# A graph network on one core: a sort's products one step behind their one-hots, and a gather loop in written order

## The chip, the core and the metric

The kernel runs on one core of a Trainium2 chip. The metric is the time of one launch in device microseconds, shown as the median of several runs. The engines are named as in the profile: PE (TensorE matmuls; PEld its weight loads), DVE (VectorE), ACT (ScalarE), POOL (GpSimd, which here issues the indirect DMAs), SP (SyncE, which issues most other DMAs). Each engine works through a queue of its own in a fixed order and waits on semaphores for the others.

## What is computed

A network of eight layers over 6250 nodes of 256 features and 100,000 edges (131,072 in one layer). Only the two layers around the change matter. Layer 3 adds up, for each node, a transformed feature row of every neighbour:

```python
def _L1_gnn_ref(vertex_features, edge_index, w0, w1):
    w0_features = vertex_features @ w0
    w1_features = vertex_features @ w1
    dst, src = (edge_index[0], edge_index[1])
    messages = w1_features[src]
    neighbours = jax.ops.segment_sum(messages, dst, num_segments=vertex_features.shape[0])
    return jax.nn.relu(w0_features + neighbours)
```

Layer 1 is an attention over the same edges (a softmax over each node's incoming edges), and layer 4 a graph attention over another list of 131,072 edges. The edges of layers 3 and 4 come in an order that does not suit the sums, so the kernel sorts each list by blocks of 128 nodes ("buckets") while an earlier layer runs.

## The kernel before

**The program.** `build` calls the eight stages one after the other. A scheduler orders the instructions of PE, DVE, ACT and SP from its own cost model; inside a `manual_schedule` block the engines named there keep the order in which the source writes them. Before the change such blocks stand around the loops of stages 1 and 5 and name POOL alone (`ORDERED`, L35); stage 3 has none.

**The sort, `bucket_move` (from L147).** It is a generator: each `yield` ends a step, and the stage that hosts it calls `next` (its "tick") between pieces of its own work. The sort of layer 3's edges (`sb`, 125 partitions x 800 columns) rides on stage 1, whose loop goes over 112 windows of 896 edges; the sort of layer 4's edges (`sc`, 128 x 1024) rides on stage 3. Its parts:
- Preparation: keys and values are loaded and cut into parts of 7 and 10 bits (one step).
- Counts (L223 to L229): the columns go in halves of 512 (L212). For each of 49 buckets DVE makes a 0/1 tile `isb` of 512 columns (L217, two buffers) and PE adds it into one row of `cnt` (L225).
- Positions (L297 to L310): for each bucket and half, DVE makes `isb`, PE forms three products into the PSUM tile `small` (L302 to L304, two buffers), and DVE copies the result into `pos` where the key fits (L307), one step late.
- Products (L333 to L351), in groups of 114 or 115 columns: for each 6 (`sc`) or 4 (`sb`) columns DVE makes the one-hots `ol` (L339) and `orr` (L341), multiplies the values into `orr` (L344, two instructions), and PE forms one product for each column into `mv` (L347). `ol` and `orr` have two buffers. Between groups `mv` is turned into rows, and POOL scatters them to DRAM (`scatter`, L326), 16 DMAs a group, one a step.
- The end (from L394): the sorted list is read back in pieces of 128 rows, turned by PE (L407) and written to `sl`, which the stage that uses the list reads.

**Stage 3 (`stage3`, from L1062).** A first loop computes `wd`, the neighbours' rows, as three bf16 parts, and `acc`. The second loop (L1097 to L1115) goes over 448 chunks of 256 edges. A chunk has one bucket b, which DVE's sequencer loads into a register eight at a time (`buckets`, L638). For a chunk, POOL issues two gathers of 128 rows (L630 through `gather`, tile `row3`, six buffers); PE adds the rows to the lanes of their nodes by six products with the one-hots `sel` (L1112, tile `nbp`, two PSUM buffers); DVE adds the result to `acc` (L1115). `sel` is made by DVE for four chunks at a time (L1103, two buffers). Each pass of the loop begins with one step of the sort. Behind the loop the remaining steps run, and DVE adds relu(acc) to X, 49 instructions.

Of the kernel before, what the change touches and what calls it, by code (L numbers as in the profile page):

```python
# [8 lines left out]
F = mybir.dt.float32  # L9
# [11 lines left out]
D = 256  # L21
# [13 lines left out]
ORDERED = {mybir.EngineType.Pool}  # L35
TOKG = [(g * 4, min(4, NT - g * 4)) for g in range((NT + 3) // 4)]
# [11 lines left out]
class Kern:  # L48
# [98 lines left out]
    def bucket_move(self, cx, keep, nm, key, oth, E, clamp=None, BT=6):  # L147
# [149 lines left out]
        held = None  # L297
        for b in range(NT):
            for h, n in halves:
                q = isb(b, h, n)  # L300
                big = small()
                nc.tensor.matmul(big[:, :n], bef, q, start=True, stop=False)  # L302
                for j in range(2):
                    nc.tensor.matmul(big[:, :n], idt[:NT, j, b:b + 1].to_broadcast([NT, 128]),  # L304
                                     first[:, j, h:h + n], start=False, stop=(j == 1))
                if held is not None:
                    nc.vector.copy_predicated(*held)  # L307
                held = (pos[:, h:h + n], q.bitcast(I16), big[:, :n])
                yield
        nc.vector.copy_predicated(*held)  # L310
# [22 lines left out]
        for g, c0, n in groups:  # L333
            mv = pp.tile([128, 2, W], F, name="mv")
            for c in range(c0, c0 + n, BT):
                k = min(BT, c0 + n - c)
                spread = lambda v, m: v[:, c:c + k].unsqueeze(1).to_broadcast([128, m, k])
# [8 lines left out]
                for i in range(k):  # L346
                    nc.tensor.matmul(mv, ol[:, :, i], orr[:, 0:2, :, i], start=(c + i == c0),  # L347
                                     stop=(c + i == c0 + n - 1))
# [1771 lines left out]
```

## Time and profile before

| what | us |
|---|---|
| median of 3 runs | 11024.03 |
| lowest, highest | 10996.14, 11024.14 |
| the profiled execution's own time | 10998.23 |
| its span | 10996.5 |
| stage 1's windows, first to last gather | 388.6 to 2274.6 |
| stage 3's loop, first gather to last add | 3527.1 to 5057.4 |
| stage 4's attention loop, first to last gather | 5181.2 to 7016.1 |

Busy time over the span: PE 6591.2 us (60%), PEld 4291.3 (39%), DVE 5176.0 (47%), POOL 4554.3 (41%), ACT 2132.4 (19%). No engine is full over the span, since the stages have different limits; a stage must be read by itself. In a line of a group of instructions the first number behind the bar is the group's busy time, the second the mean length of one in ns, and behind the next bar stands how long the engine was idle just before them and what ended the wait. "issue" means that nothing which the profile shows was waited for, "remote" that what ended the wait isn't told.

### The profile page before, as it was taken

The numbers are of one execution on the slowest core, as the hardware profiler recorded it, in microseconds if no ns is written. First come the engines' busy times: TensorE is split into PE (matmuls) and PEld (weight loads), VectorE is DVE, ScalarE is ACT, GpSimd is POOL, SyncE is SP. The second block draws the span as 40 slices with busy tenths as digits, with TensorE's granted clock in tenths as the row PEclk, the third lists the DMA queues.
The fourth block names the chain that finished last, engine by engine and source line by source line (L and its number), as shares of the span: only waits on it lengthen the run. The fifth ranks groups of instructions, "written<-read, shape, count | busy, mean of one in ns | idle before, by whom it ended". The sixth has DMA issues, their size and how long they took to land. (4 is left out here: it accounts for less than half of the span.)

```text
span 10996.5 us, 110782 instructions
## 1 busy us (share of the span) xinstructions
PE 6591.2 (60%) x33267; PEld 4291.3 (39%) x33267; DVE 5176.0 (47%) x14399; ACT 2132.4 (19%) x6797; POOL 4554.3 (41%) x4496
## 2 busy tenths in 40 slices
PE   4787767524784776664555556496455652742494
PEld 1344445413662333333233333275244441531363
DVE  5568855466314455543555555512333337333304
ACT  1243346420232000000111111122111110211120
POOL 0245656410133666773444444124266661243211
PEclk9888778765897776665565556588777785776597
DMA  3443356532662443343000000055444442452222
GB/s 129 150 135 110 108 154 195 152 113 90 197 200 94 136 121 100 105 115 75 7 7 6 6 7 7 4 189 179 112 118 118 123 115 75 147 161 49 53 74 69
DMA packets 613968, 1128.65 MB, mean 103 GB/s; under 512 B 156477, under 2 KB 420222, under 8 KB 599270
## 3 DMA queue, kind: packets, MB, share of 16 engines
q0 software_dynamic: 234752, 600.59, 20.7%
q1 hardware_dynamic: 320167, 454.29, 13.7%
q10 hardware_dynamic: 58412, 66.25, 2.0%
q8 instruction: 281, 4.60, 0.2%
q14 instruction: 356, 2.92, 0.1%
HBM read 930.96 MB, written 189.76 MB: 102 GB/s over the span
## 5 line engine op out<-in xcount | busy, mean ns | idle before, releaser
L765 PE MATMUL ops<-roww,ow 128*128 128x260 f32 (+1 forms) x3136 | 1025.1, 476 | 480.8 <-issue 236.7
L630 POOL DMA_INDIRECT roww<-kvd,saidx x784 | 843.2, 1076 | 1023.5 <-PE small L225 385.9
L630 POOL DMA_INDIRECT row<-gatd,scsl x864 | 834.6, 966 | 1001.4 <-issue 220.7
L630 POOL DMA_INDIRECT row<-w1d,sbsl x896 | 892.4, 996 | 568.8 <-PE nbp L1112 178.4
L630 POOL DMA_INDIRECT roww<-zd,saidx x784 | 811.1, 1035 | 587.0 <-issue 220.9
L765 PEld LDWEIGHTS ops<-roww,ow 128*128 128x128 f32 x3136 | 712.9, 242 | 690.0 <-issue 276.0
L1112 PE MATMUL nbp<-row,sel 128*128 128x256 bf16 x2688 | 576.9, 364 | 329.3 <-DMA row<-w1d,sbsl 201.1
L753 ACT ACTIVATE roww<-roww,pw 128x64 f32<-128x64 f32 x3136 | 758.4, 333 | 18.1 <-issue 15.6
L1514 DVE TENSOR_REDUCE Mc<-P 128x4 f32<-128x1024 f32 x432 | 520.7, 1221 | 375.0 <-remote 221.1
L347 PE MATMUL mv<-orr,ol 128*128 128x234 f16 (+1 forms) x1824 | 545.8, 445 | 216.1 <-DVE orr L344 171.3
L1029 PE MATMUL qe<-qw,ohT 128*128 128x256 bf16 x2352 | 424.5, 319 | 303.7 <-DVE roww L1032 214.7
L1112 PEld LDWEIGHTS <-sel 128*128 128x128 bf16 x2688 | 371.1, 155 | 583.7 <-issue 325.6
L1510 PE MATMUL P<-identb,mb 128*128 128x512 bf16 x864 | 470.2, 566 | 166.7 <-issue 86.8
L1351 PE MATMUL yp<-wr,hr 128*128 128x256 f32 x2176 | 537.8, 387 | 52.7 <-DVE yr L1354 52.4
L1389 PE MATMUL hp<-xr,wr 128*128 128x256 f32 x2176 | 535.3, 398 | 28.4 <-ACT hr L1391 18.0
L1354 DVE TENSOR_TENSOR yr<-yp,br 128x256 f32<-128x256 f32 x328 | 138.8, 424 | 862.4 <-PE yp L1351 797.5
L1148 PE MATMUL tps<-ident,xn 128*128 128x128 f32 x490 | 125.5, 404 | 686.3 <-DVE xn L125 470.7
L1513 PE MATMUL P<-rb,sel 96*128 96x512 bf16 x864 | 468.5, 565 | 88.2 <-DVE rb L1504 70.5
L1032 DVE TENSOR_TENSOR roww<-roww,qe 128x512 f32<-128x512 f32 x448 | 270.3, 612 | 399.5 <-DMA roww<-kvd,saidx 166.2
L1389 PEld LDWEIGHTS hp<-xr,wr 128*128 128x128 f32 x2176 | 400.3, 196 | 143.5 <-ACT hr L1391 28.0
L1351 PEld LDWEIGHTS yp<-wr,hr 128*128 128x128 f32 x2176 | 408.9, 194 | 109.0 <-DVE yr L1354 57.6
L1115 DVE TENSOR_TENSOR acc<-acc,nbp 128x256 f32 x448 | 187.2, 418 | 523.3 <-PE nbp L1112 313.1
(587 smaller groups left out, 12967.4 us busy)
## 6 DMA issues: line engine op xcount, KB each, us to landing
wr<-in_moe_dram SPq DMA_DIRECT2D x108, 1026.0 KB
lr<-salaned SPq DMA_DIRECT2D x112, 448.0 KB
yd<-yr SPq DMA_DIRECT2D x164, 256.0 KB
wr<-in_moe_dram SPq DMA_DIRECT2D x56, 513.0 KB
eat<-in_edge_attr_dram ACTq DMA_DIRECT2D x32, 781.2 KB
qw<-qd SPq DMA_DIRECT2D x112, 192.0 KB
br<-in_L_ffn_b_dram SPq DMA_DIRECT2D x164, 128.0 KB
main<-osb SPq DMA_DIRECT2D x112, 129.0 KB
```

Source lines behind the costliest of these rows:

```text
L347: nc.tensor.matmul(mv, ol[:, :, i], orr[:, 0:2, :, i], start=(c + i == c0), stop=(c + i == c0 + n - 1))
L630: return self.nc.gpsimd.indirect_dma_start(out=out, out_offset=None, in_=table, in_offset=bass.IndirectOffsetOnAxis(ap=idx, axis=0))
L753: nc.scalar.activation(x, x, AF.Copy, scale=p[:, j, i * H + h:i * H + h + 1])
L765: nc.tensor.matmul(ps[:, :VW], ow[:, j, :], row[:, j, v0:v0 + VW], start=(j == 0), stop=(j == BW - 1))
L1029: nc.tensor.matmul(ps[:, b], ohT[:, j + b, :], qw[:, k], start=(k == 0), stop=(k == 2))
L1032: nc.vector.tensor_mul(kr, kr, ps[:, :m])
L1112: nc.tensor.matmul(ps, sel[:, :, 2 * (c % G) + k], row[:, j * D:(j + 1) * D], start=(k + j == 0), stop=(k == 1 and j == 2))
L1351: nc.tensor.matmul(yp, hT[:, k, i * 128:(i + 1) * 128], w[:, O2 + k * D:O2 + (k + 1) * D], start=(k == 0), stop=(k == KH - 1))
L1389: nc.tensor.matmul(hp, w[:, k * H + m * 128:k * H + (m + 1) * 128], xe[:, k], start=(k == 0), stop=(k == 1))
L1510: nc.tensor.matmul(P[:, k], mb[:, :, 2 * i + k], self.identb.unsqueeze(1).to_broadcast([128, 4, 128]), start=True, stop=False)
L1513: nc.tensor.matmul(P[:, k], sel[:, 2 * i + k, :], rb, start=False, stop=True)
L1514: nc.vector.tensor_reduce(mg[:, i, :], P.rearrange("p k h e -> p h k e"), AX.XY, ALU.max)
```

## The change

Four edits go together.

The sort's products stand one step behind their one-hots. In the counts two buckets' one-hots are made in a step and multiplied in the next; in the positions PE's three products follow a step behind `isb`, and DVE's copy another step behind; in the groups `moved` issues the products of the step before. `isb` gets three buffers and the halves are equal (400 + 400 columns for `sb`, where they were 512 + 288). There are two more steps in the positions and one more in each group.

Stage 3's loop stands in a `manual_schedule` block that names POOL, PE, DVE and ACT. In a pass it now issues the chunk's two gathers, loads the buckets, lets the sort do a step, forms the six products, and then adds the sums of the chunk before (`held`). `sel` is made in the second pass of the four before those that use it (`hot`).

A row tile holds both gathers of a chunk and has five buffers: ten gathers where there were six.

```diff
+ORDER3 = ORDERED | {mybir.EngineType.PE, mybir.EngineType.DVE, mybir.EngineType.Activation}
...
-        halves = [(h, min(512, C - h)) for h in range(0, C, 512)]
+        HW = -(-C // -(-C // 512))
+        halves = [(h, min(HW, C - h)) for h in range(0, C, HW)]
...
-            q = wp.tile([128, 512], H16, name="isb")
+            q = wp.tile([128, HW], H16, name="isb", bufs=3)
...
-            for b in range(NT):
-                nc.tensor.matmul(big[:NT, :n], ko[:, NT - 1 - b:2 * NT - 1 - b], isb(b, h, n),
-                                 start=(b == 0), stop=(b == NT - 1))
-                if b % 2:
-                    yield
+            due = []
+            for b in range(NT + 1):
+                if len(due) > 1 or b == NT:
+                    for a, q in due:
+                        nc.tensor.matmul(big[:NT, :n], ko[:, NT - 1 - a:2 * NT - 1 - a], q,
+                                         start=(a == 0), stop=(a == NT - 1))
+                    due = []
+                if b < NT:
+                    due.append((b, isb(b, h, n)))
+                    if b % 2:
+                        yield
...
-        held = None
-        for b in range(NT):
-            for h, n in halves:
-                q = isb(b, h, n)
+        held, due = None, None
+        for b, h, n in [(b, h, n) for b in range(NT) for h, n in halves] + 2 * [(NT, 0, 0)]:
+            if held is not None:
+                nc.vector.copy_predicated(*held)
+                held = None
+            if due is not None:
+                a, i, m, q = due
                 big = small()
...
+                held = (pos[:, i:i + m], q.bitcast(I16), big[:, :m])
+            due = (b, h, n, isb(b, h, n)) if b < NT else None
+            yield
...
+            def moved():
+                for i in range(due[3]):
+                    at = due[2] + i
+                    nc.tensor.matmul(mv, due[0][:, :, i], due[1][:, 0:2, :, i], start=(at == c0),
+                                     stop=(at == c0 + n - 1))
+
             for c in range(c0, c0 + n, BT):
                 k = min(BT, c0 + n - c)
+                if due is not None:
+                    moved()
...
-                for i in range(k):
-                    nc.tensor.matmul(mv, ol[:, :, i], orr[:, 0:2, :, i], start=(c + i == c0),
-                                     stop=(c + i == c0 + n - 1))
+                due = (ol, orr, c, k)
                 if c > c0:
                     scatter(1)
                 yield
+            moved()
+            yield
...
-                gp = cx.enter_context(tc.tile_pool(name="s3g", bufs=6))
+                gp = cx.enter_context(tc.tile_pool(name="s3g", bufs=5))
...
+                with tc.manual_schedule(engines=ORDER3):
+                    nxt, held = hot(0), None
+                    for c in range(NCH):
+                        if c % G == 0:
+                            sel = nxt
+                        row = gp.tile([128, 2, 3 * D], BF, name="row3")
+                        for k in range(2):
+                            self.gather(row[:, k, :], wdf, S["idx"][:, 2 * c + k, 0:1])
+                        b = self.buckets(S, c)
+                        next(steps, None)
+                        ps = pp.tile([128, D], F, name="nbp")
+                        for k in range(2):
+                            for j in range(3):
+                                nc.tensor.matmul(ps, sel[:, :, 2 * (c % G) + k], row[:, k, j * D:(j + 1) * D],
+                                                 start=(k + j == 0), stop=(k == 1 and j == 2))
+                        if held is not None:
+                            add(*held)
+                        held = (ps, b)
+                        if c % G == 1:
+                            nxt = hot(c - 1 + G)
+                    add(*held)
+                    for _ in steps:
+                        pass
```

`hot(c)` makes the `sel` of four chunks as L1103 did, `add(ps, b)` adds a chunk's sums to `acc` as L1115 did.

More of the change, by code (lines that the diff above doesn't have):

```diff
@@ L295, in bucket_move @@
         yield
-        held = None
-        for b in range(NT):
-            for h, n in halves:
-                q = isb(b, h, n)
+        held, due = None, None
[5 more added lines that the diff above has]
+                a, i, m, q = due
                 big = small()
-                nc.tensor.matmul(big[:, :n], bef, q, start=True, stop=False)
+                nc.tensor.matmul(big[:, :m], bef, q, start=True, stop=False)
                 for j in range(2):
[L304 to L310, printed above, removed]
+                    nc.tensor.matmul(big[:, :m], idt[:NT, j, a:a + 1].to_broadcast([NT, 128]),
+                                     first[:, j, i:i + m], start=False, stop=(j == 1))
+                held = (pos[:, i:i + m], q.bitcast(I16), big[:, :m])
+            due = (b, h, n, isb(b, h, n)) if b < NT else None
+            yield
         nc.vector.tensor_copy(ki, pos)
@@ L334, in bucket_move @@
             mv = pp.tile([128, 2, W], F, name="mv")
+            due = None
+            def moved():
[3 more added lines that the diff above has]
+                                     stop=(at == c0 + n - 1))
             for c in range(c0, c0 + n, BT):
                 k = min(BT, c0 + n - c)
+                if due is not None:
+                    moved()
                 spread = lambda v, m: v[:, c:c + k].unsqueeze(1).to_broadcast([128, m, k])
@@ L1096, in stage3, with hot @@
                 steps = routes(cx)
-                for c in range(NCH):
-                    next(steps, None)
-                    b = self.buckets(S, c)
-                    if c % G == 0:
-                        n = 2 * min(G, NCH - c)
-                        sel = sp.tile([128, 128, 2 * G], BF, name="sel")
-                        nc.vector.tensor_tensor(
-                            sel[:, :, :n], iog[:, :, :n],
-                            locb[:, 2 * c:2 * c + n].unsqueeze(1).to_broadcast([128, 128, n]),
-                            ALU.is_equal)
-                    ps = pp.tile([128, D], F, name="nbp")
-                    for k in range(2):
-                        row = gp.tile([128, 3 * D], BF, name="row3")
-                        self.gather(row, wdf, S["idx"][:, 2 * c + k, 0:1])
-                        for j in range(3):
-                            nc.tensor.matmul(ps, sel[:, :, 2 * (c % G) + k], row[:, j * D:(j + 1) * D],
-                                             start=(k + j == 0), stop=(k == 1 and j == 2))
+                def hot(c):
+                    if c >= NCH:
+                        return None
+                    n = 2 * min(G, NCH - c)
+                    sel = sp.tile([128, 128, 2 * G], BF, name="sel")
+                    nc.vector.tensor_tensor(
+                        sel[:, :, :n], iog[:, :, :n],
+                        locb[:, 2 * c:2 * c + n].unsqueeze(1).to_broadcast([128, 128, n]), ALU.is_equal)
+                    return sel
@@ L1114, in stage3, with add @@
+                def add(ps, b):
                     ab = acc[:, ds(b, 1), :].rearrange("p o d -> p (o d)")
                     nc.vector.tensor_add(ab, ab, ps)
-                for _ in steps:
-                    pass
+                with tc.manual_schedule(engines=ORDER3):
[21 more added lines that the diff above has]
+                        pass
```

## The prediction

> **What bounds the kernel now.** I read the list of groups first, then stage 3 alone (its loop over 448 chunks runs from the first gather at 3527.05 us to the last add at 5057.4 us, 1530.4 us of a span of 10996.5 us), stage by stage, and then a few microseconds of its timeline. The groups inside the loop (line, engine, operation, count; then busy us, mean ns of one; then the engine's idle time before them and what ended it):
>
> ```profile
> L630 POOL DMA_INDIRECT row<-w1d,sbsl x896 | 892.4, 996 | 568.8 <-PE nbp L1112 178.4 <-issue 165.8 <-DVE ko L177 137.8
> L347 PE MATMUL mv<-orr,ol 128*128 128x234 f16 x1024 | 347.3, 493 | 93.3 <-DVE orr L344 59.2 <-issue 31.5 <-DVE acc L1115 2.3
> L1115 DVE TENSOR_TENSOR acc<-acc,nbp 128x256 f32 x448 | 187.2, 418 | 523.3 <-PE nbp L1112 313.1 <-remote 127.0 <-issue 41.5
> L326 POOL DMA_INDIRECT scsld<-vt,ti x144 | 153.1, 1063 | 43.9 <-issue 42.3 <-DVE orr L344 0.6 <-DVE acc L1115 0.3
> ```
>
> POOL issues 1,040 indirect DMAs here, and no engine has more work in a row: 892.4 + 153.1 us. (The 137.8 us wait lies before the loop.) Next the four parts of the loop: the sort's counts, its positions, its products, and the rest. Columns: length; busy us and instructions of PE, PEld, DVE, ACT, POOL; granted clock; DMA share; GB/s.
>
> ```profile
> 3527.00:3700.00 173.00, 116.96 (x465) 55.20 (x465) 80.93 (x243) 1.18 (x2) 122.90 (x122) 0.72 0.50 144
> 3700.00:3965.00 265.00, 203.28 (x832) 92.22 (x832) 136.27 (x299) 0.00 (x0) 175.06 (x183) 0.74 0.49 137
> 3965.00:4850.00 885.00, 615.88 (x2491) 338.21 (x2490) 478.08 (x1075) 4.95 (x18) 619.59 (x606) 0.65 0.38 104
> 4850.00:5062.00 212.00, 104.62 (x399) 59.45 (x399) 51.14 (x150) 0.00 (x0) 128.72 (x133) 0.50 0.60 124
> ```
>
> The timeline of the products shows how the time beside that work is lost:
>
> ```profile
> 4309.02 0.95 POOL L630 DMA_INDIRECT row<-w1d,sbsl  x1 [0.30 <-issue]
> 4310.27 0.95 POOL L630 DMA_INDIRECT row<-w1d,sbsl  x1 [0.30 <-issue]
> 4310.99 0.56 DVE L339 TENSOR_TENSOR ol<-iot,rl 128x768 f16<-128x768 f16 x1 [1.42 <-PE mv L347]
> 4311.90 0.68 DVE L1103 TENSOR_TENSOR sel<-iog,locb 128x1024 bf16<-128x1024 bf16 x1
> 4312.64 1.93 PE L1112 MATMUL nbp<-row,sel 128*128 128x256 bf16 x8 [0.92 <-DVE sel L1103]
> 4313.77 0.96 POOL L630 DMA_INDIRECT row<-w1d,sbsl  x1 [2.56 <-PE nbp L1112]
> ```
>
> Undisturbed gathers follow each other with 0.30 us between them (first two lines). Then DVE waits for PE's products to free a one-hot buffer, so sel comes late, so PE's sums come late, so no row buffer is free, and POOL, the engine with most to do, stands 2.56 us. With 0.30 us on each of POOL's instructions its own need is, part by part, 122.9 + 36.6 = 159.5 of 173; 175.06 + 54.9 = 230.0 of 265; 619.59 + 181.8 = 801.4 of 885; 128.72 + 39.9 = 168.6 of 212: together 1359.5, and 175.5 us in which it stands.
>
> **Part 1: stage 3 in written order, ten row buffers, adds one chunk late.** No instruction of the loop's work is taken away or added: 896 gathers, 144 scatters, 2,688 sums, 1,024 products, 448 adds and 112 sels stand in the built order of both. What can go is POOL's 175.5 us. Is anything else near POOL's pace? In the product part a step with a scatter costs POOL 2 x (470.53/466 + 0.30) + 1.063 + 0.30 = 3.98 us, one without 2.62 us (16 of a group's 26 steps have one). DVE needs 0.555 (ol) + 3 x 0.52 (orr) + 0.42 (acc) + 0.68/4 (sel) = 2.7 us. PE needs 2.08 us for six products (as at 4305.22) and 0.84 us (fast clock, 4307.11) to 1.44 us (slow clock, 4946.90) for six sums: 2.9 to 3.5 us. In the written order each PE step reads one-hots made a step earlier, and DVE's add reads sums made a chunk earlier; no wait has its releaser in the same step. PE's queue is products of step s-1, sums of chunk c; behind a late row wait only the next step's products, and for these DVE's next-but-one one-hots. So POOL sets the pace there. I take 75 of its 83.6 us. In the positions POOL needs 2 x (0.957 + 0.30) = 2.5 us a chunk and PE 3 x 0.48 + 0.84 to 1.44 = 2.3 to 2.9 us against 2.9 us now (265/91): PE is as near as POOL, and I take 18 of 35. In the opening I take 7 of 13.5. In the last part 9.2 us of the 43.4 are the way from the last gather to the last add, which stays; DMA share reaches 0.80 in the last 60 us at 109 GB/s, where deeper buffers may not help; I take 20 of the other 34. Sum: 75 + 18 + 7 + 20 = **120 us**.
>
> The wait that no view shows is POOL's wait with ten row buffers. Lower bound: only the product part's waits for PE sums go, 77.2 - 93 x 0.30 = 49 us. Upper: all but the last 9.2 us, 166 us. 120 is nearer the upper one because 104 us (178.4 - 248 x 0.30) of all the standing is put down to PE's sums directly, and 15 us more to other PE groups.
>
> Ten buffers hold about five chunks, 12.5 us of gathers, where six held 7.5. They must cover stalls such as this one, in which PE and DVE both stood for lack of something the profile does not name:
>
> ```profile
> 4547.30 0.42 DVE L1115 TENSOR_TENSOR acc<-acc,nbp 128x256 f32 x1 [10.88 <-remote]
> 4548.65 2.05 PE L347 MATMUL mv<-orr,ol 128*128 128x234 f16 x6 [9.49 <-issue]
> 4548.99 0.94 POOL L630 DMA_INDIRECT row<-w1d,sbsl  x1 [3.05 <-issue]
> ```
>
> A 10.9 us stall costs POOL 3.05 us with six buffers and should cost nothing with ten. If the rows come late for another reason, this cover is gone and the lower bound holds.
>
> Gathers beside more DVE work may be longer. The rows don't say so: with DVE 47, 51, 54 and 24% busy in the four parts, one gather (the first and last with a few other instructions among them) took 122.9/122 = 1.007, 0.957, 1.010 and 128.72/133 = 0.968 us. If all were at 1.010 the 896 would cost 0.014 us each over their mean of 0.996, 13 us; I take 5.
>
> The Trainium skill (SBUF — State Buffer, section Who interferes with whom) speaks against a denser DVE: a DVE instruction in a two-port mode shuts POOL out for its whole length, and POOL then can't write its descriptors. Taken to the letter for this loop's one-source 16-bit one-hots, 196 isb x 0.28 us, up to 55 us of POOL time would be at stake, but they are there before as well, so the sum by the rule would not change.
>
> **Part 2: the sort has more steps.** Before: 1 + 48 + 4 + 98 + 1 + 9 x 25 + 4 + 4 + 9 x 7 = 448, one for each chunk. After: positions 100, groups 26: 459. Eleven steps run behind the last chunk: about ten DVE operations of 0.28 us and two transposes on PE, among them the last of scsl. They stand among the 48 adds into X; **+3 us**, 0 to 8. In stage 1 nine steps more end the sort about one window later; it ends at 1582 us there and nobody reads it before stage 3: 0. At the start of the loop the first add stands behind ten DVE operations of 0.7 to 1.2 us and PE's third chunk behind it; POOL has ten buffers to fill in that time: 0, or 8 us without that cover.
>
> **Part 3: the same lag in stage 1.** There the sort rides on 57 of 112 windows. The 690 us of its products, in the columns of above, and two lines of their waits (us in all, times, longest us):
>
> ```profile
> 790.00:1480.00 690.00, 485.13 (x2721) 324.56 (x2718) 548.08 (x1213) 259.50 (x1028) 404.81 (x314) 0.79 0.40 111
> PE mv L347 <- DVE orr L344: 112.0, 60, 12.9
> DVE ol L339 <- PE mv L347: 12.4, 18, 3.3
> ```
>
> DVE is 79% busy and PE waits for DVE, hardly the reverse. A PE that is a step late frees PE, not DVE. What DVE can gain is its own 12.4 us; the 112 us of PE count only where PE is behind. The other engines keep the scheduler's order, and in the built program PE's products stand no further behind DVE's one-hots than before. **-10 us**, between +20 and -40. Halves of 400 + 400 for 512 + 288 are the same columns: 0.
>
> **Part 4: what the scheduler re-draws.** The built order also differs in stage 4 (its inputs scsl are ready later in the scheduler's eyes). No instruction is added. Its reductions idle 375 us in 432 calls; a tenth either way is +-37 us; I take 0.
>
> **Sum.** Against the profiled execution's 10998.23 us: -120 + 5 + 3 - 10 = -122, so 10876 us. That execution lies 26 us below the median of the runs shown (11024.03; lowest 10996.14). I forecast **10880 us** for the median.
>
> **The rivals.**
> (A) *Half the gain*: PE takes POOL's place. Its weight loads waited 325.6 + 217.8 us for "issue", which no buffer of rows mends, and at the slow clock it needs 2.9 us in the positions and 3.5 us in the products. For: clock 0.65 in the products. Against: 3.98 us on POOL where scatters go. Time: 49 us of stage 3, none of stage 1: 10998 - 49 + 8 = 10957. Chance 0.17.
> (B) *All of it*: POOL never stands (166), stage 1 gives 30: 10805. Chance 0.08.
> (C) *Nothing*: the sums wait for rows in flight (201.1 us put down to the row DMA), so the order in which they are awaited does not matter. Against it, POOL's waits are put down to PE's sums and not to DMAs. 10990. Chance 0.09.
> (D) *Slower*: the unnamed stalls grow. DVE's "remote" waits over 1 us are 40, 162.9 us in all; if they are supply that queues behind gathers in flight, ten rows in flight for six could double them, and in written order a stalled DVE soon stops PE too. Then -122 + 163 = +41: 11039. It decides from a growth of 95% on (155 us, to be 33 over). Chance 0.08.
> My forecast: 0.58.
>
> **How the numbers follow.** What a measurement of this kernel can tell from no change is about 0.3%, 33 us. Faster: forecast, A and B, 0.83. Same: C, 0.09. Slower: D, 0.08. My forecast's own range is 10835 to 10930 (the re-drawn stages). To leave out no more than 0.2 it reaches up over A to 10975 and down to B's 10800.
>
> **What would show it.** Right: the loop's length near 1410 us; POOL's gathers idle mostly 0.30 us each and waits for PE's sums well below 60 us; the product part near 3.5 us a chunk, not 3.8. Part 2: scsl's last writes among the adds into X. Part 3: the window rate in stage 1 as before. Wrong: PE's sums with no gap before them at a clock of 0.5 (A); DVE "remote" or PE "issue" waits far over 163 and 108 us (D); stage 4 longer or shorter by over 37 us.

## The result and the profile after

The changed kernel takes 11162.2 us (median of four runs, 11155.05 to 11181.94) against 11024.08 us (four runs, 10996.14 to 11027.43): 1.0134 times as long, 95% interval 1.0112 to 1.0156. Forecast were 10880 us. The profiled execution took 11155.05 us, its span is 11153.3 us, 157 us more than before. By stages (first to last gather; for stage 3 to the last add):

| stage | before, us | after, us | change | forecast |
|---|---|---|---|---|
| 1, windows | 388.6 to 2274.6 (1886.0) | 389.0 to 2417.9 (2028.9) | +143 | -10 |
| 3, loop | 1530.4 | 1526.0 | -4 | -120 |
| 4, attention loop | 5181.2 to 7016.1 (1835) | 5327.0 to 7172.9 (1846) | +11 | 0 |

Nearly the whole loss lies in stage 1, where a gain of 10 us was forecast, and the gain of stage 3 did not come. The groups of after that answer to those shown of before (columns as there; the second line counts both sorts):

```profile
L650 POOL DMA_INDIRECT row<-w1d,sbsl x896 | 890.6, 994 | 535.5 <-issue 229.9 <-DVE pos L194 138.5 <-remote 105.4
L350 PE MATMUL mv<-orr,ol 128*128 128x234 f16 (+1 forms) x1824 | 549.4, 444 | 276.8 <-DVE orr L364 210.5 <-issue 62.7 <-DVE roww L1052 2.9
L1130 DVE TENSOR_TENSOR acc<-acc,nbp 128x256 f32 x448 | 186.8, 417 | 462.7 <-remote 235.8 <-PE nbp L1146 123.1 <-PE small L316 36.1
L336 POOL DMA_INDIRECT scsld<-vt,ti x144 | 154.0, 1070 | 66.2 <-issue 41.7 <-DVE ti L408 23.5 <-DVE outp L406 0.7
```

In the first line PE's sums no longer stand among the releasers, where 178.4 us were put down to them; "remote" stands there now with 105.4 us. In the third, DVE's adds wait 123.1 us for PE's sums, not 313.1, and 235.8 us for "remote", not 127.0. The waits went from a name to no name and the loop kept its length. Products and scatters are as long as before (444 and 1070 ns; 445 over both sorts and 1063 before). The loop's four parts after (counts, positions, products, rest):

```profile
3673.60:3831.40 157.80, 92.46 (x411) 45.06 (x412) 64.99 (x205) 1.18 (x2) 105.15 (x109) 0.73 0.49 137
3831.40:4122.50 291.10, 218.81 (x907) 101.21 (x906) 152.27 (x341) 0.00 (x0) 194.90 (x203) 0.70 0.49 137
4122.50:4970.00 847.50, 573.91 (x2419) 321.89 (x2418) 475.71 (x1039) 4.39 (x16) 599.34 (x580) 0.67 0.39 106
4970.00:5200.00 230.00, 105.01 (x451) 66.04 (x450) 58.36 (x155) 0.55 (x2) 145.97 (x150) 0.55 0.58 119
```

The parts begin at other chunks, so they are compared per chunk: counts 2.89 us before and 2.92 after, positions 2.90 and 2.88, products 3.79 and 3.75, the rest 3.35 and 3.43. With 0.30 us on each instruction POOL's need is 137.9, 255.8, 773.3 and 191.0 us; it stands for the other 168.4 us, where it stood 175.5 us before.

In stage 1 the same stretch of time, 1600 to 1950 us, where the sort is over and the windows run alone. Before:

```profile
1600.00:1950.00 350.00, 264.77 (x1654) 177.86 (x1654) 194.47 (x284) 226.47 (x921) 215.53 (x204) 0.88 0.65 199
```

And after:

```profile
1600.00:1950.00 350.00, 201.43 (x1225) 145.26 (x1223) 152.59 (x218) 169.89 (x680) 142.81 (x145) 0.77 0.48 147
```

POOL issues 145 gathers where it issued 204, seven a window: 16.9 us a window for 12.0. No engine is more than 58% busy and the DMA share is lower than before, so the time goes into waiting for one another. Window 56 of 112, a little behind the sort's end, begins at 1511.8 us after and 1509.3 us before; the loss is in the windows behind it, and window by window in these eight-window means (us a window):

| windows | 56-64 | 64-72 | 72-80 | 80-88 | 88-96 | 96-104 | 104-112 |
|---|---|---|---|---|---|---|---|
| before | 12.36 | 11.20 | 12.36 | 12.66 | 14.22 | 16.89 | 17.15 |
| after | 12.49 | 16.59 | 16.98 | 17.11 | 17.02 | 17.10 | 17.14 |

Windows 64 to 96 lose 8 x (5.39 + 4.62 + 4.45 + 2.80) = 138 us. Before, too, the last windows run at 17 us.

The sort's products in stage 1 after, first the stretch and then two lines of its waits (us in all, times, longest us):

```profile
790.00:1480.00 690.00, 453.03 (x2556) 301.44 (x2554) 510.12 (x1118) 245.09 (x963) 372.83 (x299) 0.77 0.38 105
```

```profile
PE mv L350 <- DVE orr L364: 117.6, 56, 14.3
DVE ol L359 <- PE mv L350: 24.2, 16, 9.9
```

The wait of DVE that the lag was to remove grew from 12.4 to 24.2 us; PE's stayed (112.0, 117.6). The lag gained nothing in these two waits.

**The order behind the 17 us.** Where the windows run alone, the programs as built differ in where the scheduler put PE's work. PE makes, for each pair of windows, 42 products of rows (qe, L1049), 28 turns, and 14 sums (ops, L785; the profile records each as two matmuls, so the x14 below is one window's seven sums) of an earlier pair. Counted in the traces, with the pairs numbered from 0: in the quick order the sums of pair p's first window end behind 18 of the 42 row products of pair p + 2, and the second window's begin behind 41 of them. In the slow order they stand behind 7 and 21 row products of pair p + 3. Six row tiles (`rows=6`) hold three pairs, so a window of pair p + 3 can gather its rows only when the sums of pair p have freed a tile: in the slow order the second window's sums wait for rows whose place the first window's sums have only just freed. The slow order holds in pairs 46 to 52 before and in pairs 31 to 52 after, with mixed forms in the two pairs ahead of each; the expectations below count 9 and 27 pairs where the traces show these 7 and 22. What it does (the timeline of after, one turn):

```profile
2016.96 0.39 ACT L790 ACTIVATE osb<-ops 128x260 f32<-128x260 f32 x1 [1.39 <-PE ops L785]
2017.19 0.94 POOL L650 DMA_INDIRECT roww<-kvd,saidx  x1 [7.81 <-PE ops L785]
...
2017.37 0.26 SPq L814 DMA_DIRECT2D main<-osb  x1
...
2024.75 0.94 POOL L650 DMA_INDIRECT roww<-kvd,saidx  x1 [0.30 <-issue]
2025.95 0.69 DVE L1052 TENSOR_TENSOR roww<-roww,qe 128x512 f32<-128x512 f32 x1 [7.33 <-DMA roww<-kvd,saidx]
2026.70 1.46 PE L1049 MATMUL qe<-qw,ohT 128*128 128x256 bf16 x6 [9.23 <-DVE roww L1052]
...
2029.10 4.72 PE L785 MATMUL ops<-roww,ow 128*128 128x260 f32 x14
...
2033.86 0.39 ACT L790 ACTIVATE osb<-ops 128x260 f32<-128x260 f32 x1 [15.66 <-PE ops L785]
...
2034.56 1.21 POOL L650 DMA_INDIRECT roww<-kvd,saidx  x1 [8.87 <-ACT osb L790]
```

It is a ring: sums end, row buffers come free and POOL issues seven gathers (2017.19 to 2025.7); DVE has stood 7.33 us for these rows, PE 9.23 us for DVE; then come the row products, then the sums, and only then the next gathers. A turn is one window; POOL stands 8.87 us of its 17.

### The profile page after: what moved, and what is told of

Read it like the earlier page. It is cut to its first block, busy times and chain, and to the rows that moved or that the text cites. A ratio compares the mean times of both kernels' runs of the same rounds, so it can differ in the third digit from the quotient of the medians.

```text
span 11153.3 us, 110204 instructions
## 1 busy us (share of the span) xinstructions
PE 6536.9 (59%) x33267; PEld 4302.8 (39%) x33267; DVE 5194.2 (47%) x14399; ACT 2139.0 (19%) x6797; POOL 4526.8 (41%) x4496
## 3 DMA queue, kind: packets, MB, share of 16 engines
q14 instruction: 353, 2.89, 0.1%
## 5 line engine op out<-in xcount | busy, mean ns | idle before, releaser
L785 PE MATMUL ops<-roww,ow 128*128 128x260 f32 (+1 forms) x3136 | 1040.7, 481 | 463.5 <-issue 257.5
L650 POOL DMA_INDIRECT roww<-kvd,saidx x784 | 820.4, 1046 | 1142.3 <-PE small L231 386.3
L785 PEld LDWEIGHTS ops<-roww,ow 128*128 128x128 f32 x3136 | 726.9, 247 | 661.0 <-issue 281.6
L1146 PE MATMUL nbp<-row,sel 128*128 128x256 bf16 x2688 | 538.9, 351 | 340.8 <-DVE acc L1130 174.0
L1049 PE MATMUL qe<-qw,ohT 128*128 128x256 bf16 x2352 | 439.8, 323 | 487.0 <-DVE roww L1052 334.4
L1049 PEld LDWEIGHTS <-ohT 128*128 128x128 bf16 x2352 | 254.9, 114 | 653.8 <-issue 343.0
## 6 DMA issues: line engine op xcount, KB each, us to landing
main<-osb SPq DMA_DIRECT2D x112, 129.0 KB
```

The source lines that it names most:

```text
L650: return self.nc.gpsimd.indirect_dma_start(out=out, out_offset=None, in_=table, in_offset=bass.IndirectOffsetOnAxis(ap=idx, axis=0))
L785: nc.tensor.matmul(ps[:, :VW], ow[:, j, :], row[:, j, v0:v0 + VW], start=(j == 0), stop=(j == BW - 1))
L1049: nc.tensor.matmul(ps[:, b], ohT[:, j + b, :], qw[:, k], start=(k == 0), stop=(k == 2))
L1146: nc.tensor.matmul(ps, sel[:, :, 2 * (c % G) + k], row[:, k, j * D:(j + 1) * D], start=(k + j == 0), stop=(k == 1 and j == 2))
```

## The experiments

The runs were made in groups; each group ran on one chip beside runs of the kernel before, so a ratio is comparable within its group. The kernel before took 11139.02 and 11133.17 us in the groups on one chip, and 10188.44, 10199.26 and 10192.35 us on three others. "Pace" is the time of a window in stage 1 behind the sort (windows 64 to 88).

**Which edit slows stage 1: the lag or an order?** Three kernels, each the changed one but for one edit (before: 11139.02 us). The first has the old sort, without the lag, in stage 1:

```diff
-    K.stage1(by_dst, lambda cx: K.bucket_move(cx, K.keep, "sb", A["src"], A["dst"], E0, BT=4))
+    K.stage1(by_dst, lambda cx: K.bucket_move_old(cx, K.keep, "sb", A["src"], A["dst"], E0, BT=4))
```

> The changed kernel, with the sort on stage 1 in its old form (no lag, halves 512 + 288, two isb buffers); stage 3 as changed. Theory Order: stage 1 lost its 143 us not to the lag itself but to the order of PE's queue, in which the window sums (ops) stand behind the next windows' qe products. In the built order of this kernel 23 of 56 pairs of windows (30 to 52) stand so, against 9 in the kernel before and 27 in the changed one; a pair in that order costs 2 x 4.7 us more, so 11024 + 14 x 9.4 = about 11155 us. Theory Lag: the sort's late products themselves hold up stage 1; with the old sort it is as before, and with stage 3 at -4 us the kernel takes about 11020 us.

Measured: 11293.44 us, 1.013 (1.0093 to 1.0167), pace 17.06 us. The loss stays without the lag in stage 1.

The second has stage 3's loop of before, with six buffers and no block, and keeps the new sort:

```diff
-                with tc.manual_schedule(engines=ORDER3):
-                    nxt, held = hot(0), None
...
+                for c in range(NCH):
+                    next(steps, None)
```

> The changed kernel with stage 3's loop as it was before (scheduler's order, six single-row buffers); both sorts with the lag. Theory Order: only 8 pairs of windows in stage 1 (45 to 52) have the slow order in the built program; 14 more stand in an order of a third kind, in which the sums come between the qe products of the next pair. If that is as fast as before, about 11020 us; at most 11024 + 14 x 9.4 = 11155 us if it is as slow. Theory Lag: the lag is in here, so stage 1 is 143 us longer: about 11165 us.

Measured: 11202.07 us, 1.0053 (1.0035 to 1.0072), pace 13.8 to 15.7 us: a third order, between the two, with a smaller loss. So the edits in stage 3 alone move stage 1, two stages earlier in the program, and the new sort without stage 3's block moves it too.

The third takes PE's order in stage 1 out of the scheduler's hands:

```diff
-            with tc.manual_schedule(engines=ORDERED):
+            with tc.manual_schedule(engines=ORDERED | {mybir.EngineType.PE}):
                 self.att_windows(cx, S, kvd, 512, 4, 256, load, front, main, part, ends, rows=6, steps=steps)
```

> The changed kernel, and in stage 1 PE's instructions stand in the order of the source too. Then every pair has the sums of the pair before between the two windows' qe products. Theory Order: no pair pays the 4.7 us a window of the slow order, so from 11162 us 27 pairs x 9.4 = 254 us go, about 10910 us (10880 to 10960), and the windows after the sort run at 12.3 us or less to the end. Theory Lag, or that the windows are held by something else than PE's order (rows that land late, DVE): 11130 us or more.

Measured: 11318.4 us, 1.0161 (1.0119 to 1.0203). Missed. The order was not the one that the expectation names: in the trace all 14 sums of a pair stand behind all 42 row products of the next, and PE waits for ACT between the two windows' sums (6.24 us at 2026.84). Alone the windows take 15.4 us; that this order is the reason was not tested. Beside the sort they are slower: window 56 begins at 1630.6 us, and at 1552.0 us with the old sort on the same chip.

**What re-draws it?** (before: 10188.44 us.) The first is the kernel before with its own loop of stage 3 inside a block that names DVE alone:

```diff
-                for c in range(NCH):
-                    next(steps, None)
...
+                with tc.manual_schedule(engines={mybir.EngineType.DVE}):
+                    for c in range(NCH):
+                        next(steps, None)
```

> The kernel before, and one thing more: stage 3's loop stands in a manual_schedule block that names DVE alone. Nothing of stage 1, of the sorts or of the buffers is edited. In the built program pairs 30 to 52 of stage 1's windows then have the slow order on PE (the held windows' sums behind 27 and 41 of the next pair's 42 qe products; before this began at pair 44). Theory Order: the windows 60 to 88 run at 17.05 us instead of 12.4, so 14 pairs x 9.4 = +132 us, ratio 1.012 (1.009 to 1.015). Theory Lag (stage 1 lost its time to the sort's late products): stage 1 as before, ratio 1.000 (0.996 to 1.004).

Measured: 10371.67 us, 1.0179 (1.0158 to 1.02). Stage 1's windows take 1874.5 us, at a pace of 16.97 to 17.07 us. Stage 3's loop is longer too, 1468.4 us against 1416.5 us in the order of before on that chip (from the trace of the kernel below with sums written earlier in stage 1), which was not expected; so the ratio is above the range that stage 1 accounts for.

The second is the changed kernel with the old sort in stage 1 and without DVE in stage 3's block:

```diff
-                with tc.manual_schedule(engines=ORDER3):
+                with tc.manual_schedule(engines=ORDERED | {mybir.EngineType.PE, mybir.EngineType.Activation}):
```

> The changed kernel with stage 1's sort in its old form, and DVE is not named in stage 3's block (Pool, PE and ACT are). In the built program stage 1's PE order is that of the kernel before, pair by pair. Theory Order: stage 1 as before, ratio 1.000 (0.996 to 1.004), with stage 3 at 1510 to 1550 us. If stage 1's loss came from the ten row buffers, the written order of PE or the lag in the other sort, the windows after the sort stay at 17 us: ratio 1.013.

Measured: 10175.41 us, 0.9989 (0.9979 to 0.9999); stage 1 takes 1738.2 us at 12.3 to 12.6 us, as forecast; stage 3 takes 1397.2 us, well under the 1510 to 1550 expected. The same 200 us of both, first with DVE named:

```profile
1558.00:1758.00 200.00, 113.93 (x676) 83.30 (x677) 82.82 (x119) 93.44 (x375) 79.96 (x81) 0.74 0.47 141
```

And without:

```profile
1558.00:1758.00 200.00, 145.13 (x926) 98.69 (x925) 111.98 (x164) 126.08 (x514) 121.96 (x115) 0.88 0.63 195
```

81 gathers against 115, and 136 us of stage 1 between the two (1874.5 and 1738.2 us). The second run names POOL, PE and ACT in stage 3's block and has the ten buffers and stage 3's new sort, and in its trace PE's order of sums and row products in the windows alone is, pair for pair, that of the kernel before; so none of these needs to move stage 1. From the kernel with the old sort in stage 1 above, which has a pace of 17.06 us on another chip, it differs by the name DVE alone. Why the scheduler draws an earlier stage otherwise when DVE is named later stays open: its inner workings were not looked into.

**Do earlier sums help?** (same group.) If the slow order's fault is that sums stand late, sums put early should give more than the quick order. Two ways, on the kernel before: with a higher priority for the scheduler, and written earlier.

```diff
+                with tc.high_priority():
-                weigh(held)
-                scaled(held, 0)
+                    weigh(held)
+                    scaled(held, 0)
...
+                with tc.high_priority():
-                for i in range(held["n"]):
-                    sums(held, i)
+                    for i in range(held["n"]):
+                        sums(held, i)
```

> The kernel before, with the scheduler's priority raised for the held pair's weights, scalings and sums in stage 1 (weigh, scaled of the first window, sums); same instructions. In the built order the first window's sums then stand behind about 14 to 24 of the next pair's qe products and the last ones behind 36 at most. Theory Order: no pair has the slow order (9 had it), the windows go at 12.4 us or less to the end: 9 x 9.4 = -85 us, ratio 0.992 (0.988 to 0.996). If the 17 us of the last pairs has another cause (rows, the end of the sort): ratio 1.000 or more.

```diff
                 scaled(held, 0)
+                sums(held, 0)
...
                     scaled(held, 1)
-                for i in range(held["n"]):
-                    sums(held, i)
+                    sums(held, 1)
```

> The kernel before, with the first held window's sums written ahead of the next qe products and the second's right behind its scalings; no priority is raised, same instructions. In the built order the sums of both windows stand spread among the next pair's 30 qe products, the last ones behind 36 at most in the last pairs. Theory Order: ratio 0.992 (0.988 to 0.997), as with the raised priority. Otherwise 1.000 or more.

Measured: 10319.34 us, 1.0134 (1.0104 to 1.0164), and 10198.3 us, 1.0003 (0.9989 to 1.0018). Both missed. The pace is 11.8 to 12.7 us, as before, and the last pairs are slow in both (15.6 to 16.6 us). In the traces the pairs up to 41 and 43 have the first window's sums end behind 14 row products of pair p + 2 with the priority and behind 26 when written earlier (18 before), and the last pairs stay in a slow order in both, so neither run shows what an early order to the end would give. With the priority stage 1 took 1776.0 us, 37 more than the 1739.3 of the other, in an execution of 10253.22 us that lies 66 us under its median; where its remaining loss lies was not followed up.

**What holds the ring up?** In the landing records of after's slow turns 15 of a gather's 16 parts land within some 1 us, and the sixteenth 2.0 us later (both medians, windows 64 to 87). At the same time the store of the sums is on the way (from the list of DMA issues of after):

```profile
main<-osb SPq DMA_DIRECT2D x112, 129.0 KB
```

129.0 KB are 127 rows of 1040 bytes, and its records stand one behind the other, some 18 per us, some 7 us for all. The Trainium skill (DMA: Bandwidth & Descriptors, section "Why a DMA increments its semaphore by 16 and not by 1") says that a DMA uses the largest number of engines up to 16 that divides the slowest dimension of both of its sides, one for 127 partitions. The records agree: the rows of the store follow each other at 44 ns and take 47 ns each (medians), which is one at a time. The edit splits the store into 112 and 15 rows:

```diff
-                nc.sync.dma_start(main[1:NP + 128, :][ds(r[i], 127), :], o[1:128])
+                nc.sync.dma_start(main[1:NP + 128, :][ds(r[i], 112), :], o[1:113])
+                nc.sync.dma_start(main[113:NP + 128, :][ds(r[i], 15), :], o[113:128])
```

Three kernels have it (before: 11133.17 us): the changed one, the one before, and the changed one with the old sort in stage 1 and without DVE named.

> The changed kernel, but each window's 127 rows of sums go to DRAM in two DMAs of 112 and 15 rows instead of one of 127 (stages 1 and 5, 112 windows each). PE's order in the built program is that of the changed kernel. Theory Chain: in the slow order the next rows are gathered only when a window's sums are done, and are waited for at once; the store of these sums starts at the same moment, its 1040-byte packets run in one row of 17 in a microsecond (so one of the DMA engines does all 127), and the last of the 16 parts of each gather lands 2.1 to 2.4 us behind the fifteenth. With the store spread, the first wait for rows shortens by that: 17.05 us a window becomes 14.5 to 15.5, over some 54 windows 80 to 130 us, ratio to the kernel before 1.002 to 1.008 instead of 1.0134. If the late sixteenth part has nothing to do with the store, or the rows are not on the chain: 1.011 to 1.016.

> The kernel before with the same split store. Theory Chain: its last 22 windows are in the slow order, 2 us less each, 45 us, and the others and stage 5's 112 windows gain something between 0 and 1 us each: ratio 0.990 to 0.997. Otherwise 1.000, or more if the 224 further DMA issues on SP stand in the way of its loads.

> The split store on the version with the old sort in stage 1 and DVE not named in stage 3's block (0.9989 of the kernel before without the split). If both gains add: ratio 0.988 to 0.996, the fastest so far. Otherwise 0.999.

Measured: 11239.71 us, 1.0085 (1.0068 to 1.0102), pace 15.8 to 16.2 us; 11110.39 us, 0.9985 (0.9972 to 0.9998), pace 11.6 to 11.9; 11048.71 us, 0.9922 (0.9903 to 0.994), pace 11.5. The sixteenth part now lands 0.1 us behind the others, so the store was what delayed it. In the slow order that gave 0.9 us a window where 1.5 to 2.5 had been expected, and the ratio missed its range (1.002 to 1.008); the second's ratio missed too (0.990 to 0.997). The store was a part of the ring, not its cause. Only the second has a kernel without the split in its own group; the other two gains compare ratios of different chips.

**Why did stage 3 not gain?** First, if PE's sums at a low clock hold it, a third of them should show (group of 11139.02 us):

```diff
                         for k in range(2):
-                            for j in range(3):
-                                nc.tensor.matmul(ps, sel[:, :, 2 * (c % G) + k], row[:, k, j * D:(j + 1) * D],
-                                                 start=(k + j == 0), stop=(k == 1 and j == 2))
+                            nc.tensor.matmul(ps, sel[:, :, 2 * (c % G) + k], row[:, k, 0:D],
+                                             start=(k == 0), stop=(k == 1))
```

> The changed kernel, but stage 3 adds up only the first of the three bf16 parts of each gathered row: two products a chunk where there were six; gathers, adds and sort are the same. Theory Clock: stage 3's loop is bounded by PE at the clock that it is granted (0.69 of full in this loop, with a stop of PE of 3 to 5 us at nearly each step down of the clock, and the adds that wait for it). With 4 of 6 sums gone, 0.5 to 1.0 us of PE a chunk, the loop falls from 1526 us towards POOL's own need of 1360 us: loop 1370 to 1440 us, kernel about 11010 to 11080 us. Theory Rows: the loop waits for rows in flight or for POOL and DVE; then the loop stays at 1500 to 1530 us and the kernel at 11140 to 11165 us.

Measured: 11262.56 us, 1.011 (1.0062 to 1.0158), loop 1512.4 us against 1539.8 to 1550.3 us for the others of the group. With two thirds of PE's sums gone the loop is 1.8 to 2.4% shorter. But PE's busy time in the loop fell by some 200 us only, since the granted clock fell as well (first the loop of the kernel with the old sort in stage 1, whose stage 3 is the changed one, on the same chip; then the loop of this one):

```profile
3724.40:5274.80 1550.40, 1009.73 (x4184) 538.27 (x4184) 750.35 (x1737) 6.14 (x20) 1045.92 (x1042) 0.65 0.44 115
3711.10:5223.60 1512.50, 806.73 (x2392) 296.65 (x2392) 745.27 (x1737) 6.12 (x20) 1047.55 (x1042) 0.51 0.45 118
```

So 203 us of PE's time are worth 38 us of the loop, and PE's work is not what holds it. The waits are still there:

```profile
L1130 DVE TENSOR_TENSOR acc<-acc,nbp 128x256 f32 x448 | 186.2, 416 | 303.4 <-remote 136.0 <-PE nbp L1145 97.2 <-issue 24.8
```

What they are, the timeline of the changed kernel shows:

```profile
3887.90 0.88 PE L1146 MATMUL nbp<-row,sel 128*128 128x256 bf16 x6
...
3889.46 0.88 PE L1146 MATMUL nbp<-row,sel 128*128 128x256 bf16 x6
...
3892.39 0.95 POOL L650 DMA_INDIRECT row<-w1d,sbsl  x1 [0.30 <-issue]
3893.95 0.42 DVE L1130 TENSOR_TENSOR acc<-acc,nbp 128x256 f32 x1 [3.34 <-remote]
3894.19 0.94 POOL L650 DMA_INDIRECT row<-w1d,sbsl  x1 [0.85 <-remote]
3894.43 0.80 PE L1146 MATMUL nbp<-row,sel 128*128 128x256 bf16 x3 [2.85 <-issue]
```

DVE's add at 3893.95 takes the sums that PE ended at 3888.78 (first line); PE's signal is recorded at 3893.93, five us later. DVE, POOL and PE all stand until then. The granted clock steps from 1.0 to 0.5 inside this stall, at 3892.4 us, so a stop of PE at such a step is a rival. It can't make most of these waits: of the two loops shown above the first has 50 steps down and 164 waits over 0.3 us put down to "remote", the second 5 steps down and still 157. Over the span, all engines together, the trace of before has 394 such waits, 1916 us in all, nearly all of them (1879 us) for a signal of PE, and that of after 480, 2626 us. On the three chips where the kernel before takes 10188 to 10199 us no wait over 0.3 us is put down to "remote". To see the change without such waits, the changed kernel was run again, unedited, beside one that gathers a third of the bytes, in case the bytes make the signals late (it also has the single product of the diff above; before: 10199.26 us):

```diff
-                            self.gather(row[:, k, :], wdf, S["idx"][:, 2 * c + k, 0:1])
+                            self.gather(row[:, k, 0:D], wd.rearrange("n j d -> (n j) d"), S["idx"][:, 2 * c + k, 0:1])
```

> The changed kernel once more, unedited, beside the kernel before on one chip. Theory Order with Late completions: stage 1 loses 4.7 us in some 27 to 30 windows whatever the chip (ratio 1.012 to 1.018). Stage 3 depends on the chip: where PE's signals come late (DVE's remote waits in the loop, 127 us in the first profile, none in the group of runs where the kernel before took 10188 us), the loop takes 1500 to 1550 us in every order; where none come late, it falls to POOL's own need, 1360 to 1400 us, against 1416 us for the old order there. Theory Written order: stage 3's written order itself holds the loop at 1500 us or more on every chip.

> As s3_third_sums (two products a chunk), and the gathers read 512 bytes of a row where they read 1536; they take them at a third of the distance, so they are other rows: the sums of stage 3 are other numbers. Gathers, adds and sort are as many as before. Theory Traffic: PE's late signals and the loop's 2.9 us a chunk come from the rows' bytes (135 GB/s); with a third of them the loop falls to 1360 to 1430 us on any chip. Theory Chip: late signals come from PE's side of the chip and not from the bytes; then the loop stays at 1490 to 1530 us where DVE has remote waits, and is at 1360 to 1400 us where it has none.

Measured: 10278.18 us, 1.0072 (1.0045 to 1.01), loop 1382.6 us; and 10266.47 us, 1.0059 (1.0038 to 1.008), loop 1386.7 us. No signal was late on this chip, so the second says nothing on bytes and late signals. It does say that here neither the bytes nor PE's clock hold the loop: with a third of the bytes, and PE at half clock as in the run above, the loop is as long as the first's.

```profile
3478.30:4865.00 1386.70, 849.60 (x2392) 281.18 (x2392) 762.28 (x1737) 6.12 (x20) 1044.27 (x1042) 0.50 0.23 44
```

The first says a good deal:

```profile
L650 POOL DMA_INDIRECT row<-w1d,sbsl x896 | 888.8, 992 | 423.4 <-issue 220.5 <-DVE pos L194 136.4 <-DMA row<-w1d,sbsl 32.3
L1130 DVE TENSOR_TENSOR acc<-acc,nbp 128x256 f32 x448 | 187.1, 418 | 342.5 <-PE nbp L1146 341.3
```

"Remote" is gone from both lines. Its four parts:

```profile
3486.30:3625.20 138.90, 93.61 (x417) 45.72 (x418) 65.55 (x207) 1.18 (x2) 106.13 (x110) 0.81 0.55 156
3625.20:3882.50 257.30, 207.57 (x911) 96.01 (x909) 158.72 (x351) 0.00 (x0) 196.07 (x204) 0.81 0.56 155
3882.50:4651.60 769.10, 639.25 (x2428) 335.13 (x2427) 484.60 (x1044) 4.42 (x16) 592.40 (x581) 0.60 0.43 117
4651.60:4868.90 217.30, 114.61 (x434) 61.91 (x431) 51.85 (x138) 0.55 (x2) 144.43 (x150) 0.52 0.58 126
```

With 0.30 us on each instruction POOL needs 139.1, 257.3, 766.7 and 189.4 us: in the first three parts it stands for 2.4 us in all. Stage 1 is slow here as well (15.7 to 17.07 us), which is why the kernel still loses.

**A version that beats both.** (before: 10192.35 us.) If naming DVE in stage 3 re-draws stage 1, DVE's order in stage 1 can be written down too:

```diff
-            with tc.manual_schedule(engines=ORDERED):
+            with tc.manual_schedule(engines=ORDERED | {mybir.EngineType.DVE}):
                 self.att_windows(cx, S, kvd, 512, 4, 256, load, front, main, part, ends, rows=6, steps=steps)
```

The first kernel is the changed one with this; the second has the split store besides; the third is the second with the old sort in stage 1.

> The changed kernel, and stage 1's block names DVE beside Pool: DVE keeps the order of the source there too. In the built program all pairs from 30 on have one order on PE, in which the first held window's sums stand behind the 20 products of the pair's own second window and the second's behind 21 of the next pair's 42 (slow order: 27 and 41). Theory Chain (rows are gathered only after the held sums, which wait for the next pair's rows): with no row of the next pair's second window on that way the last 50 windows run at 12.4 us or less to the end: 54 x 4.7 = 254 us under the changed kernel's, ratio 0.985 to 0.995; on a chip whose loop in stage 3 has no late signals 0.980 to 0.990. If a strict DVE order costs as much as PE's did (15.4 us a window, and 100 us during the sort): 1.01 or more.

> The same with the split store (112 + 15 rows). If it adds as it did to the changed kernel (1.0134 to 1.0085) or to no_dve (0.9989 to 0.9922): 0.003 to 0.007 lower than after_s1_dve. If the rows are no longer waited for: the same.

> The same as after_s1_dve_split with stage 1's sort in its old form: what the lag is worth in stage 1 when PE's order in the windows after the sort is the same. Where DVE's order is fixed, a product that follows its one-hots in the same step holds PE for them; Theory Lag helps: this one is 0.002 to 0.010 above after_s1_dve_split. If the lag does nothing: the same.

Measured: 10073.79 us, 0.988 (0.9864 to 0.9897), pace 12.24 to 12.45 us to the very end; 9941.29 us, 0.9758 (0.974 to 0.9777), 9.9 to 10.1 us to the end; 9946.49 us, 0.976 (0.9743 to 0.9776). In the traces PE's order is now one in which the first window's sums end behind the 42 row products of pair p + 1 and the second's behind 21 of pair p + 2, in every pair from 27 to 53: no sum waits for a row that needs a tile of its own pair. 350 us of the second kernel:

```profile
1550.00:1900.00 350.00, 280.53 (x1947) 196.37 (x1948) 235.69 (x341) 266.76 (x1073) 275.36 (x246) 0.97 0.80 241
```

POOL issues 246 gathers and with 0.30 us on each needs 349.2 of the 350 us: in stage 1 now, too, it sets the pace. The lag of the sort's products is worth nothing measurable in stage 1 (0.9758 and 0.976). The split store gives here what it did not give in the slow order, some 12.3 to 10.0 us a window; stage 5, whose store it splits as well, keeps its time (1083.8 and 1080.4 us from first to last gather).

## Why the prediction was wrong, step by step

**Part 3 and part 4: the step that failed.** Part 3 put stage 1 at -10 us, "between +20 and -40", and the sign that was to show it was "the window rate in stage 1 as before". It went from 12 to 17 us a window, +143 us. The sentence behind it, "in the built program PE's products stand no further behind DVE's one-hots than before", looked at the sort's products only; the windows' own sums, which run for some 690 us behind the sort (1582 to 2274.6 us), were not compared. Part 4, "what the scheduler re-draws", counted stage 4 and left out stage 1, though a scheduler that orders one stage anew may order any. The order of PE in the traces shows it: pairs 31 to 52 in the slow order where there had been 46 to 52. The price also stood in the trace of before, whose last 16 windows take 17 us: the prediction did not ask why. Had the step been "15 pairs more in the slow order", 15 x 2 x (17.05 - 12.3) = 142 us would have been the estimate for the measured 143. The cause is shown down to one name that suffices: DVE in stage 3's block, without any of the other edits, gives +136 us in stage 1. The lag gives nothing where PE's order is the same, but it is not without effect on the order: with the new sort and without the block a third order came out, at 1.0053.

**Part 1: a second step that failed, a reason right and a gain that another wait took.** POOL's waits for PE's sums went from 178.4 to 18.0 us, "well below 60" as forecast, but the loop is 4 us shorter, not 120. The premise that failed is the one named in "If the rows come late for another reason, this cover is gone and the lower bound holds": what comes late is PE's signals, not rows, and the cover is gone, but even the lower bound of 49 us was too high. With the sums' wait gone, the late signals ended the stalls instead (POOL's gathers waited 47.0 us for "remote" before, 105.4 after); that is read from the releasers in the two traces, since no run could take the late signals away on that chip. On a chip without late signals POOL runs at its own need up to the last part of the loop, as the step said. The size is open even so: there the loop takes 1382.6 us, against 1416.5 us in the old order on another such chip: 34 us less, not 120, and 19 us less on one and the same chip with the written order of POOL, PE and ACT alone (1397.2 us). Without late signals the old order stands only 57 us above POOL's need (1359.5 us, from the prediction's sum), so there was less to take.

**Gathers beside more DVE work**, +5 us: mean 994 ns for 996, nothing. **Part 2**, +3 us: the 49 adds into X that follow the last chunk begin within 18.6 us of each other for 16.2 before, +2, inside its 0 to 8, and scsl's last writes stand among them, as it said. **The sum** took -122 from the profiled execution and then gave 10880 us for the median, which lies 26 us higher; from the median it makes 10902. Against a miss of 282 us this weighs little.

**The rivals.** D said that unnamed stalls could double, and they did: DVE's "remote" waits over 1 us in the loop went from 40, 162.9 us, to 88, 344.4 us. Yet the loop did not grow, so D was right in its mark and wrong in its price; and its cause, ten rows in flight for six, isn't shown. That the kernel is slower, as D had it, is luck: its loss is in another stage. A, PE in POOL's place, fell with the two runs at half clock: 203 us less of PE gave 38, and on the other chip the loop took 1386.7 us, near POOL's need, with PE at a clock of 0.50. B's "POOL never stands" came nearly true on another chip for three parts of four. C's time was close for stage 3 and its reason, rows in flight, wrong: PE's sums waited 201.1 us for rows before and 76.6 us after, and the loop kept its length. None of them had a loss in stage 1; it was a case that was not listed.

What stays open: what makes PE's signals late on some chips, and whether the loop of the first chip would reach POOL's need without them; why naming DVE in a later block re-draws stage 1; why the last windows fall back into the slow order before the change; and whether more row buffers would cut the ring in stage 1, which wasn't tried.

## What to carry to other kernels

Where a scheduler orders part of a program, compare the built order of every stage before and after an edit, not only of the stage that the edit is in; a stage whose instructions are the same lost 8% here (1738.2 to 1874.5 us). A wait that goes away is a gain only if nothing else ended the same stall: put the unnamed waits beside the named ones before counting. And when a loop turns at a pace that no engine accounts for, follow one turn as a ring; here the changed kernel with a better order gained 1.2% on the kernel before, the split store alone 0.2%, and both together 2.4%.

## What was not expected of the hardware

- On the chips of the prediction's runs and of two groups, signals from PE are recorded, and acted on by other engines, some us after the matmul's end (3888.78 to 3893.93 above; 3.2 us in the median of these waits after the change), for 1879 us of waits over the span before the change; on three others there is no such wait over 0.3 us. The ends of matmuls are modelled in the profile, so whether PE or its signal is late is not told. The kernel before takes 11024 to 11139 us on the former and 10188 to 10199 us on the latter. How much of those 8 to 9% the late signals make isn't shown.
- A store that one DMA engine carries alone delays one of the 16 parts of a gather beside it by some 2 us (median 2.0); split, 0.1 us.
- The slow order, with the store unsplit, turns at 16.98 to 17.38 us a window (eight-window means, windows 72 to 96) on each chip where it ran, with or without late signals.
